# Four planes in place of interleaved residues: output layout, send granularity, early statistics and the side of the bias

## The chip, the cores and the metric

The kernel runs on one core of a Trainium2 chip. A core has a matrix engine (PE, with its weight loads listed as PEld), three elementwise engines (DVE, ACT and POOL) and a sync engine (SP) which in this kernel issues nearly all transfers between the on-chip memory and the device memory. The metric is device time in microseconds. "Span" is the time from the first to the last instruction in one profiled execution.

## The reference

The input `x` has four images of 128 channels and 96 x 96 pixels, in float32. The layer is `x + conv(gn(x))`, where `gn` is a group norm over 32 groups. `conv` reads each image as four sequences of 9216 pixels (rows forward and backward, columns forward and backward), runs the same small network over each, and merges the four results with a 1x1 product:

```
seq_h = flat
seq_v = flat[:, :, order_v]
seq_all = concatenate([seq_h, seq_h[:, :, ::-1], seq_v, seq_v[:, :, ::-1]], axis=0)
...
t = _grouped1x1(x, in_proj_w, in_proj_b, G);  u, gate = t[:, :HID], t[:, HID:]
u = depthwise_conv5(silu(u))
s = _conv1x1(u, ssm_in_w);  a = DMIN + (DMAX - DMIN) * sigmoid(...)
bb = tanh(...);  cc = tanh(...)
hst = exp(prefix) * cumsum(bb * s * exp(-prefix));   prefix = cumsum(log(a))
u = u + _conv1x1(cc * hst + ssm_d * s, ssm_out_w)
u = _grouped1x1(u * sigmoid(gate), mix_w, mix_b, G)
y = _conv1x1(u, out_proj_w, out_proj_b)
...
out = x + einsum('oc,bchw->bohw', fuse_w, concat(h_fwd, h_rev, v_fwd, v_rev)) + fuse_b
```

So every output pixel is the input pixel plus four contributions, one a direction, plus one constant a channel.

## The kernel before, in words

**Phases, steps, pairs.** For each image `b` there are two phases: `V`, which takes the two column sequences, and `H`, which takes the two row sequences. The forward sequence is side `s = 0`, the backward one `s = 1`. A phase has six steps of 16 lines (`NS = 6`, `LN = 16`), and a step has four pairs, one for each residue of the position modulo four, in the order `TURN = (1, 2, 3, 0)`. A pair is the work of both sides for one residue of one step, 384 elements a channel (`N = 384`). There are 192 pairs, numbered `t`; the first six run in `pair(t)`, the others in `pair_on(t)`, and `tail()` ends the kernel. The order of all instructions on each engine is the order in which the program is written (a manual schedule); nothing is moved by a planner. Semaphores for data dependences are put in by the framework.

**What a pair does.** PE runs the input projection of a pair four ahead (`front`, lines 499 to 530), the depthwise convolution of half of the channels as products with banded matrices (`conv`, `conv_less`, line 130), the four small projections (`proj`, line 130), the gates (line 536), the output of the scan (line 556) and the merged output product (`accumulate`, line 130). DVE runs the convolution taps of the other half of the channels (`taps`, line 725), copies of `u` in the first six pairs (line 891), the edge term (line 672), the scan (line 800) and the gating (line 619). ACT runs the nonlinear functions and copies out of PSUM. POOL runs the small products around the scan (lines 773, 774, 806, 807, 809) and the addition into the accumulator (line 852).

**The accumulator.** `acc` holds one whole image on chip, `x` at first, and the four directions are added into it. It is laid out as lines, then residues of the column, then columns: `[P, HH, R, M]`, with `M = 24`. The host brings `x` into the same layout and turns the output back. Each unit's product goes from PSUM through ACT into a buffer `ys` (lines 833 and 835) and is added into `acc` by POOL seven pairs after the unit's own pair. In an H phase one unit's addition covers 16 lines of one residue, runs of 24 elements that lie 96 apart. In a V phase it covers all lines of one residue and four columns of each residue: 24 x 4 runs of four elements. In the H phase ACT also adds the constant of the output (`b_fin`) on side `s = 0`, in the same instruction that copies (line 833); side 1 is a plain copy (line 835). In the last pairs DVE adds straight from PSUM (lines 850, 852, 1135, 1137).

**Sends and reloads.** A block of 16 lines is finished when the second half of an H phase has added its fourth residue (`k == 3`). Then four transfers of 384 KB (two halves of each side's block, 3072 contiguous bytes a partition) go to `done`; `send()` issues them at the start of the next pair (line 815), or at the end of the pair for the last block of an image, and two pairs later (`k == 1`, or `late`, the pair in which the next image's first products are made) the same blocks of the next image's `x` are loaded (line 947). A V addition of the next image touches all lines, so it needs all of these loads. In the last step of the program the transfers are issued at the end (line 1140).

**Statistics of the next image.** The group norm of image `b + 1` is gathered during the V phase of image `b`, from chunks of 384 elements a channel which are loaded on the side into three buffers (`load_chunks`, line 424) and read by DVE (`stats_chunks`, line 430). `chunks_of(t)` says which chunks belong to pair `t`: two in each third and fourth pair of a step. The loads are issued up to two pairs ahead, as soon as a buffer is free. In `pair(t)` DVE's order is: taps of `t`, copies of `u` of `t` (line 891), scan, chunk statistics of `t`; then the taps of `t + 1`.

**The start.** The first image is loaded in chunks and its statistics are taken at once; then `keep_silu` (line 486) sends four 770 KB blocks to device memory at about the time pair 0 begins. All transfers of SP go through one queue in program order: `x_in` loads (lines 297 and 315), `edge` stores (line 657), chunks, gates.

The lines of the core of the addition:

```
        if bu["order"] == "V":
            part = acc.rearrange("p (m q) r c -> p m q r c", q=R)[
                :, :, p, :, bass.ds(st * LN // R, LN // R)
            ]
            y = y.rearrange("p (c r m) -> p m r c", r=R, m=M)
        else:
            part = acc[:, bass.ts(st, LN), p, :]
```

Of the kernel before, what the change touches and what calls it, by code (L numbers as in the profile page):

```python
# [42 lines left out]
F32 = mybir.dt.float32  # L43
# [4 lines left out]
P = 128  # L48
B, DIM, HH, WW = 4, 128, 96, 96
L = HH * WW  # L50
# [6 lines left out]
R = 4  # L57
LN = 16
NS = HH // LN
N = LN * WW // R  # L60
M = WW // R
LAG = 6
UB = 8
NP = NS * R
TURN = (1, 2, 3, 0)
# [3 lines left out]
def conv_preact_kernel(  # L69
# [14 lines left out]
    ps = ctx.enter_context(tc.tile_pool(name="psum", bufs=1, space=bass.MemoryType.PSUM))  # L84
    dp = ctx.enter_context(tc.tile_pool(name="kept", bufs=1, space=bass.MemoryType.DRAM))

    acc = big.tile([P, HH, R, M], F32, name="acc")
    accf = acc.rearrange("p h r m -> p (h r m)")
    x_in = [big.tile([P, R, N + 1], F32, name=f"x_in{s}") for s in range(2)]


# [319 lines left out]
    def chunks_of(t):  # L411

        un = units[min(2 * t, NU - 2)]
        st, k = divmod(t % NP, R)
        if un["order"] == "V" and un["b"] + 1 < B and k > 1:
            return [(un["b"] + 1, 4 * st + 2 * (k - 2) + e) for e in range(2)]
        return []

    def load_chunks(t):
        for b, c in chunks_of(t - 1) + chunks_of(t) + chunks_of(t + 1):  # L420
            if (b, c) not in loaded and len(chunks) < 3:
                loaded.add((b, c))
                chunks[b, c] = wk.tile([P, SC], F32, tag="xs", bufs=3, name=f"xs_{b}_{c}")
                nc.sync.dma_start(chunks[b, c], xr[b, :, bass.ts(c, SC)])
# [140 lines left out]
    def under(bi, s):  # L565

        if bi + s == 0:
            return
        seeded.add((bi, s))
        nc.scalar.copy(psum[:, ssm(bi, s) : ssm(bi, s) + 2, :N], us[bi][:, s])  # L570
# [239 lines left out]

    done, reload = [], []

    def send():
        for b, r in done:
            nc.sync.dma_start(out[b, :, r], accf[:, r])
            if b + 1 < B:
                reload.append((b + 1, r))
        done.clear()

    def accumulate(bu, bk, adder=nc.gpsimd, last=False):  # L820

        b, s, p, st = bu["b"], bu["s"], bu["p"], bu["st"]
        py = bank(bk)
        direct = last and (s == 1 or bu["order"] == "H")
        for j in range(2):
            for c in range(4):
                mm(py, c, w_fin[:, bu["dir"], j, 32 * c : 32 * c + 32], bu["v"][:, j, :],
                   j == 0, j == 1)
        y = py[:, :N]
        if not direct:  # L830
            ys = wk.tile([P, N], F32, tag="ys", bufs=4, name=f"ys_{bu['id']}")
            if s == 0 and bu["order"] == "H":
                nc.scalar.activation(ys, y, AF.Identity, bias=b_fin)  # L833
            else:
                nc.scalar.copy(ys, y)  # L835
            y = ys
        if s == 1:
            y, p, st = y[:, ::-1], R - 1 - p, NS - 1 - st
        if bu["order"] == "V":
            part = acc.rearrange("p (m q) r c -> p m q r c", q=R)[  # L840
                :, :, p, :, bass.ds(st * LN // R, LN // R)
            ]
            y = y.rearrange("p (c r m) -> p m r c", r=R, m=M)
        else:
            part = acc[:, bass.ts(st, LN), p, :]
            y = y.rearrange("p (h m) -> p h m", m=M)

        def add():
            if direct and s == 0:
                adder.scalar_tensor_tensor(part, y, b_fin, part, ALU.add, ALU.add)  # L850
            else:
                adder.tensor_add(part, y, part)  # L852
            if bu["order"] == "H" and bu["st"] >= NS // 2 and bu["end"]:

                done.extend((b, bass.ts(2 * st + e, LN * WW // 2)) for e in range(2))

        return add

# [57 lines left out]
    def pair_on(t):  # L916
# [23 lines left out]
            load_lone(un["step"])  # L940
        if not fronted:
            under(bi, 1)
        if t < end - 2:
            send()
        if len(reload) == 4 and (k == 1 or late):
            for b, r in reload:
                nc.sync.dma_start(accf[:, r], xr[b, :, r])
            reload.clear()
        new_u(i)
        taps(i, range(1, K))  # L950
        conv(i, banks, single)
# [99 lines left out]
    def tail():  # L1051
# [4 lines left out]
        def ssm_out(n):  # L1056
            for s in range(2):
                for j in range(2):
                    out_of(2 * n, s, j)
# [40 lines left out]
        for n in range(first + 2, end - 1):  # L1100
            gate_units(n)
            z_copy(n + 1)
            product(n - 1, 1, 5)
            add()
            product(n, 0, 4)
            ssm_out(n + 1)
        last = 2 * (end - 1)
        half = N // 2
        for s in range(2):
# [8 lines left out]
        for i, s, e in ((-2, 1, 0), (-1, 0, 0), (-1, 0, 1), (-2, 1, 1), (-1, 1, 0), (-1, 1, 1)):  # L1118
# [10 lines left out]
            if s:  # L1129
                lines = HH - lines - LN // 2  # L1130
                y = y[:, ::-1]
            part = acc[:, bass.ds(lines, LN // 2), R - 1 - bu["p"] if s else bu["p"], :]
            y = y.rearrange("p (h m) -> p h m", m=M)
            if s:
                nc.vector.tensor_add(part, y, part)
            else:
                nc.vector.scalar_tensor_tensor(part, y, b_fin, part, ALU.add, ALU.add)
            if bu["end"]:
                region = bass.ds(lines * WW, LN // 2 * WW)
                nc.sync.dma_start(out[bu["b"], :, region], accf[:, region])  # L1140

    def start():
        def filler(n):
# [185 lines left out]
```

## Time and profile before

| | us |
|---|---|
| median of three runs | 1750.28 (1747.95 to 1751.83) |
| the profiled execution's own time | 1753.03 |
| its span | 1750.9 |
| PE busy | 1724.7 |
| DVE, ACT, POOL busy | 1505.8, 1496.0, 1454.4 |

The profile page lists busy time by engine, the span in 40 slices, the transfer queues, the chain of work that ended last, and the costliest groups of instructions. Beside it stand answers of the trace: the windows view gives the busy time of every engine, the granted clock of PE and the share of the transfer engines in a stretch; the timeline lists instructions merged by line (start, time, engine, line, operation, names, count, and in brackets how long the engine had been idle and what it waited for); the view of one tile or line gives the shortest, median and longest duration, what its engine waited for, and for transfers the time from issue to landing. "L852" is line 852 of the kernel before. An engine's idle time between two instructions of 0.02 to 0.1 us is its own issue time.

### The profile page before, as it was taken

The page shows a single profiled execution, that of the slowest core. Times are in us where ns is not written, and L with a number is a line of the kernel's source. Part 1 is how long each engine was busy: PE and PEld are TensorE (multiplying, and loading weights), DVE is VectorE, ACT ScalarE, POOL GpSimd, SP SyncE. Part 2 cuts the span into 40 slices and gives each one's busy share as a digit, 9 for nine tenths or more (in the row PEclk, how much of TensorE's full clock was granted, in tenths as well). Part 3 has the DMA queues.
Part 4 walks back from the last instruction along what each step waited for, and adds up shares of the span by engine and source line. Part 5 has one row for each costly group of instructions (what it writes and reads, how often), then busy time and mean ns, then how long its engine had stood idle before and what let it go on. Part 6 is the DMA issues. An engine that isn't in the chain of part 4 may idle for free.

```text
span 1750.9 us, 54410 instructions
## 1 busy us (share of the span) xinstructions
PE 1724.7 (99%) x22662; PEld 645.5 (37%) x22662; DVE 1505.8 (86%) x1508; ACT 1496.0 (85%) x2543; POOL 1454.4 (83%) x1496
## 2 busy tenths in 40 slices
PE   7999999999999999999999999999999999999998
PEld 3233333433333333334333343334333333333333
DVE  6799988888889998888889999888888888888897
ACT  4688988889888888888888888888888888888875
POOL 3488889888879988978787998898788899887886
PEclk9999999999999999999999999999999999999999
DMA  7645965358885696337897489533897549743454
GB/s 236 198 151 186 309 197 155 116 194 262 279 270 196 230 273 191 124 117 240 256 298 260 147 290 257 159 119 132 273 279 250 196 136 294 213 139 132 147 203 181
DMA packets 164980, 362.68 MB, mean 207 GB/s; under 512 B 16640, under 2 KB 128640, under 8 KB 164736
## 3 DMA queue, kind: packets, MB, share of 16 engines
q1 hardware_dynamic: 164592, 359.17, 63.6%
q8 instruction: 179, 2.93, 0.7%
q14 instruction: 65, 0.53, 0.1%
q10 hardware_dynamic: 144, 0.04, 0.0%
HBM read 220.62 MB, written 138.53 MB: 205 GB/s over the span
## 4 chain that ended last, share of the span: by engine, by line
PE 92%; DVE 2%; POOL 2%; DMA 1%; ACT 1%; issue 1%; SPq 0%; POOLq 0%; DVEq 0%; ACTq 0%
PE psum L130 78%; PE psum L556 8%; PE psum L536 5%; DMA xs<-in_xr 1%; DVE psum L725 1%; PE psum L1144 1%; DMA acc<-in_xr 0%; POOL t L806 0%; POOL t L807 0%; DVE u L619 0%; POOL acc L852 0%; POOL t L774 0%; POOL t L773 0%; SPq L486 0%; ACT psum L570 0%
## 5 line engine op out<-in xcount | busy, mean ns | idle before, releaser
L725 DVE SCALAR_TENSOR_TENSOR psum<-sil,small,psum 128x768 f32<-128x768 f32 x576 | 589.1, 1023 | 41.4 <-ACT psum L723 16.7
L130 PE MATMUL psum<-u,w_fin 128*32 128x384 f32 (+1 forms) x6192 | 541.6, 484 | 1.0 <-ACT ys L833 0.5
L130 PE MATMUL psum<-u,main 128*32 128x384 f32 x6144 | 536.8, 490 | 2.3 <-DVE u L891 2.3
L619 DVE SCALAR_TENSOR_TENSOR u<-gate,psum 128x768 f32<-128x768 f32 x376 | 341.9, 951 | 158.2 <-ACT ys L835 59.8
L852 POOL TENSOR_TENSOR acc<-ys,acc 128x384 f32<-128x384 f32 x375 | 427.3, 1161 | 18.6 <-DMA acc<-in_xr 4.9
L806 POOL TENSOR_TENSOR t<-t,t 64x384 f32<-64x384 f32 (+1 forms) x192 | 275.6, 1435 | 70.7 <-DVE t L800 53.5
L130 PEld LDWEIGHTS psum<-u,w_fin 128*32 128x32 f32 x6192 | 195.7, 110 | 308.9 <-issue 237.9
L570 ACT COPY psum<-u 128x768 f32<-128x768 f32 x383 | 300.3, 799 | 10.4 <-DVE u L619 4.4
L130 PEld LDWEIGHTS psum<-u,main 128*32 128x32 f32 x6144 | 180.4, 110 | 327.3 <-issue 217.2
L130 PE MATMUL psum<-sil,band 128*32 128x384 f32 x3072 | 286.5, 490 | 1.1 <-ACT gate L580 1.1
L773 POOL TENSOR_SCALAR t<-tm 64x384 f32<-64x384 f32 x184 | 173.6, 943 | 117.4 <-ACT tm L762 105.4
L807 POOL TENSOR_TENSOR t<-t,t 64x384 f32<-64x384 f32 (+1 forms) x192 | 234.0, 1219 | 15.1
L723 ACT ACTIVATE psum<-sil,small 128x768 f32<-128x768 f32 x191 | 172.5, 903 | 73.4 <-DVE u L619 64.8
L774 POOL TENSOR_TENSOR t<-t,tm 64x384 f32<-64x384 f32 x192 | 210.5, 1096 | 28.6 <-ACT t L765 13.9
L556 PE MATMUL psum<-t,main 32*128 32x384 f32 x1536 | 226.9, 526 | 3.2 <-ACT psum L570 2.6
L725 DVE SCALAR_TENSOR_TENSOR u<-sil,small,psum 128x768 f32<-128x768 f32 x192 | 194.9, 1015 | 6.8
L506 ACT ACTIVATE sil<-psum,bnorm 128x385 f32<-128x385 f32 x384 | 192.0, 585 | 5.0 <-PE psum L130 2.9
L536 PE MATMUL psum<-x_in,wn 32*128 32x384 f32 x768 | 162.1, 498 | 0.0
L130 PEld LDWEIGHTS psum<-sil,band 128*32 128x32 f32 x3072 | 88.7, 108 | 173.5 <-issue 63.1
L835 ACT COPY ys<-psum 128x384 f32<-128x384 f32 x281 | 129.3, 477 | 21.7 <-PE psum L130 19.0
L762 ACT ACTIVATE tm<-psum,small 128x384 f32<-128x384 f32 x192 | 111.1, 579 | 15.7 <-PE psum L130 6.5
L574 ACT ACTIVATE gate<-psum,bnorm 128x384 f32<-128x384 f32 x152 | 88.0, 581 | 39.8 <-PE psum L536 23.4
(109 smaller groups left out, 1529.6 us busy)
## 6 DMA issues: line engine op xcount, KB each, us to landing
gate<-kept SPq DMA_DIRECT2D x114, 768.0 KB, 5.9
kept<-gate SPq DMA_DIRECT2D x74, 768.0 KB, 3.7
sil<-sil SPq DMA_DIRECT2D x64, 770.0 KB, 7.5
lone<-edge SPq DMA_DIRECT2D x39, 770.0 KB, 7.7
x_in<-in_xs SPq DMA_DIRECT2D x250, 96.2 KB, 3.4
edge<-sil SPq DMA_DIRECT2D x96, 192.5 KB, 4.3
out<-acc SPq DMA_DIRECT2D x48, 384.0 KB, 6.1
acc<-in_xr SPq DMA_DIRECT2D x39, 384.0 KB, 6.8
```

The source lines that it names most:

```text
L130: nc.tensor.matmul(o[r, : rhs.shape[-1]], lhsT, rhs, start=start, stop=stop, skip_group_check=True)
L506: nc.scalar.activation(sils[step][:, s, j, g, :], bank(bk)[:, : N + 1], AF.Silu, bias=bn[:, 1:2] if j else bn[:, 4 + g : 5 + g],)
L536: nc.tensor.matmul(bank(to)[:, :N], stats[un["b"]][0][r, s, :], x_in[s][r, q, off : off + N], start=True, stop=True)
L556: nc.tensor.matmul(bank(ssm(bi, s) + j)[:, :N], w_so[r, bass.ts(j, P)], z[r, :], start=(bi, s) not in seeded, stop=True, skip_group_check= ...
L570: nc.scalar.copy(psum[:, ssm(bi, s) : ssm(bi, s) + 2, :N], us[bi][:, s])
L619: nc.vector.scalar_tensor_tensor(v, g, 1.0, pz, ALU.add, ALU.mult)
L725: nc.vector.scalar_tensor_tensor(us[i][:, :, 1, :] if k == K - 1 else part, src, w_tap[:, k : k + 1], part, ALU.mult, ALU.add,)
L773: nc.gpsimd.tensor_scalar(*decay(i))
L774: nc.gpsimd.tensor_mul(ta[0:64, p, :], tb[0:64, :], tm[0:64, :])
L806: engine.tensor_mul(ta[0:64, p, r], tb[64:P, r], ta[64:P, p, r])
L807: engine.tensor_add(tb[0:64, r], ta[0:64, p, r], tb[0:64, r])
L852: adder.tensor_add(part, y, part)
```

## The change

The change has four parts.

1. **Layout.** `acc`, `x` and the output become four planes, one a residue of the column: `[P, R, HH, M]`. An H addition then covers 384 contiguous elements; a V addition still covers 24 x 4 runs of four elements, with the runs of one residue 96 elements apart and the residues 2304 apart (before: 384 and 24). The host's two transpositions follow.
2. **Sends and reloads.** A block is sent two planes at a time: planes 1 and 2 when `k == 1` is added, planes 0 and 3 when `k == 3` is added. Each transfer is again 384 KB, now two runs of 1536 bytes a partition. Reloads are issued at `k` of 1 or 3 and stand ahead of `send()` in a pair. In the last step of the last image single planes are sent, and in the closing block of `tail()` one plane (or half of one) each.
3. **First statistics.** In the first six pairs one chunk a pair is taken (pairs 2, 3, 4 and 5) where before two were taken in pairs 2 and 3, and only the chunk of that pair is loaded, two pairs ahead.
4. **Output's bias.** `b_fin` is added on side 1 instead of side 0, in ACT's copy and in DVE's direct additions.

```
-    acc = big.tile([P, HH, R, M], F32, name="acc")
-    accf = acc.rearrange("p h r m -> p (h r m)")
+    acc = big.tile([P, R, HH, M], F32, name="acc")
+    accf = acc.rearrange("p r h m -> p (r h m)")
...
         st, k = divmod(t % NP, R)
+        if t < LAG:
+            return [(b0 + 1, t - 2)] if t > 1 else []
...
-        for b, c in chunks_of(t - 1) + chunks_of(t) + chunks_of(t + 1):
+        ahead = chunks_of(t - 1) + chunks_of(t) + chunks_of(t + 1)
+        for b, c in ahead if t > LAG + 1 else chunks_of(t):
...
+    def planes(t, at):
+        r, lines = at
+        return t.rearrange("p (r h m) -> p r h m", r=R, m=M)[:, r, lines, :]
+
     def send():
-        for b, r in done:
-            nc.sync.dma_start(out[b, :, r], accf[:, r])
+        for b, at in done:
+            nc.sync.dma_start(planes(out[b], at), planes(accf, at))
             if b + 1 < B:
-                reload.append((b + 1, r))
+                reload.append((b + 1, at))
...
-            if s == 0 and bu["order"] == "H":
+            if s == 1 and bu["order"] == "H":
                 nc.scalar.activation(ys, y, AF.Identity, bias=b_fin)
...
-            part = acc.rearrange("p (m q) r c -> p m q r c", q=R)[
+            part = acc.rearrange("p r (m q) c -> p m q r c", q=R)[
...
-            part = acc[:, bass.ts(st, LN), p, :]
+            part = acc[:, p, bass.ts(st, LN), :]
...
-            if direct and s == 0:
+            if direct and s == 1 and bu["order"] == "H":
                 adder.scalar_tensor_tensor(part, y, b_fin, part, ALU.add, ALU.add)
...
-            if bu["order"] == "H" and bu["st"] >= NS // 2 and bu["end"]:
-
-                done.extend((b, bass.ts(2 * st + e, LN * WW // 2)) for e in range(2))
+            k = TURN.index(bu["p"])
+            if bu["order"] == "H" and bu["st"] >= NS // 2:
+                lines = bass.ts(st, LN)
+                if b + 1 == B and bu["st"] == NS - 1 and k > 1:
+                    done.append((b, (slice(p, p + 1), lines)))
+                elif k == 1:
+                    done.append((b, (slice(1, 3), lines)))
+                elif k == 3:
+                    done.append((b, (slice(0, R, 3), lines)))
...
+        if k in (1, 3) or late:
+            for b, at in reload:
+                nc.sync.dma_start(planes(accf, at), planes(xr[b], at))
+            reload.clear()
         if t < end - 2:
             send()
-        if len(reload) == 4 and (k == 1 or late):
-            for b, r in reload:
-                nc.sync.dma_start(accf[:, r], xr[b, :, r])
-            reload.clear()
...
             ssm_out(n + 1)
+        send()
...
-            if s:
+            if s == 0:
                 nc.vector.tensor_add(part, y, part)
             else:
                 nc.vector.scalar_tensor_tensor(part, y, b_fin, part, ALU.add, ALU.add)
-            if bu["end"]:
-                region = bass.ds(lines * WW, LN // 2 * WW)
-                nc.sync.dma_start(out[bu["b"], :, region], accf[:, region])
+            if s and bu["end"]:
+                at = slice(r, r + 1), bass.ds(lines, LN // 2)
+            elif e:
+                at = slice(r, r + 1), bass.ts(NS - 1 - bu["st"] if s else bu["st"], LN)
+            else:
+                continue
+            nc.sync.dma_start(planes(out[bu["b"]], at), planes(accf, at))
...
-        "xr": x.reshape(B, DIM, HH, M, R).transpose(0, 1, 2, 4, 3).reshape(B, DIM, L),
+        "xr": x.reshape(B, DIM, HH, M, R).transpose(0, 1, 4, 2, 3).reshape(B, DIM, L),
```

More of the change, by code (lines that the diff above doesn't have):

```diff
@@ L1131, in tail @@
                 y = y[:, ::-1]
-            part = acc[:, bass.ds(lines, LN // 2), R - 1 - bu["p"] if s else bu["p"], :]
+            r = R - 1 - bu["p"] if s else bu["p"]
+            part = acc[:, r, bass.ds(lines, LN // 2), :]
             y = y.rearrange("p (h m) -> p h m", m=M)
-            if s:
+            if s == 0:
                 nc.vector.tensor_add(part, y, part)
@@ L1326 @@
     r = run_bass_kernel_spmd(nc, [arrays], core_ids=[0])
-    y = r.results[0]["out_0"].reshape(B, DIM, HH, R, M)
-    return np.ascontiguousarray(y.transpose(0, 1, 2, 4, 3)).reshape(B, DIM, HH, WW)
+    y = r.results[0]["out_0"].reshape(B, DIM, R, HH, M)
+    return np.ascontiguousarray(y.transpose(0, 1, 3, 4, 2)).reshape(B, DIM, HH, WW)
```

## The prediction

> **What bounds the kernel now.** I read the page's busy times first, then the windows view by stage. The columns of the windows view are the stretch, its length, the busy time of PE, PEld, DVE, ACT and POOL, PE's granted clock, and the share and rate of the transfer engines.
>
> ```profile
> PE 1724.7 (99%) x22662; PEld 645.5 (37%) x22662; DVE 1505.8 (86%) x1508; ACT 1496.0 (85%) x2543; POOL 1454.4 (83%) x1496
> ...
> 0.00:100.00 100.00, 83.95 (x1086) 32.12 (x1086) 71.75 (x111) 59.38 (x110) 43.74 (x73) 0.97 0.74 214
> 100.00:300.00 200.00, 199.99 (x2660) 74.81 (x2656) 180.91 (x180) 175.81 (x301) 180.60 (x184) 1.00 0.62 199
> 900.00:1170.00 270.00, 268.90 (x3644) 99.52 (x3640) 243.48 (x243) 237.31 (x407) 236.76 (x240) 1.00 0.67 214
> 1700.00:1751.00 51.00, 43.16 (x528) 17.18 (x520) 37.99 (x46) 29.19 (x46) 36.58 (x35) 1.00 0.50 181
> ```
>
> PE is the bound: from 100 to 300 us it is never idle. It has 16 us of idle time in the first 100 us, 1.1 us in the stretch 900 to 1170, and 7.8 us in the last 51. The change takes nothing from PE, so it can gain only at these places, and it can lose wherever it makes another engine or a transfer slower than PE. I therefore price four places: the start, the additions on POOL, the change of image, the end. The sums are made against the profiled execution, 1753.03 us (2.1 outside its span of 1750.9); that is 2.75 above the median 1750.28, and I carry the difference over unchanged.
>
> **The start: chunks of the next image's statistics.** This is the timeline of SP, DVE and PE from 34 to 89 us, and the clock in two windows.
>
> ```profile
> 34.48 4.14 SPq L486 DMA_DIRECT2D sil<-sil  x4
> 38.66 4.31 SPq L424 DMA_DIRECT2D xs<-in_xr  x3
> 58.71 0.38 SPq L424 DMA_DIRECT2D xs<-in_xr  x1
> 59.79 2.90 SPq L297 DMA_DIRECT2D x_in<-in_xs  x4
> ...
> 52.16 1.03 DVE L430 BATCH_NORM_STATS2 bn<-xs 128x6 f32<-128x384 f32 x2 [2.54 <-DMA xs<-in_xr]
> 62.11 0.56 DVE L430 BATCH_NORM_STATS2 bn<-xs 128x6 f32<-128x384 f32 x1 [3.43 <-DMA xs<-in_xr]
> 75.03 1.02 DVE L891 COPY u<-psum 128x384 f32<-128x384 f32 x2 [1.27 <-PE psum L130]
> 84.19 1.01 DVE L672 SCALAR_TENSOR_TENSOR u<-lone,small,psum 128x768 f32<-128x768 f32 x1 [2.07 <-PE psum L130]
> ...
> 57.80 2.79 PE L130 MATMUL psum<-u,main 128*32 128x384 f32 x32 [1.62 <-DVE u L891]
> 65.69 0.99 PE L130 MATMUL psum<-x_in,wn 32*32 32x385 f32 x16 [0.82 <-DMA x_in<-in_xs]
> 67.34 4.45 PE L130 MATMUL psum<-u,main 128*32 128x384 f32 x32 [0.66 <-DVE u L891]
> ...
> 64.90:68.30 3.40, 1.95 (x28) 0.73 (x32) 3.33 (x5) 1.45 (x3) 0.00 (x0) 1.00 0.91 242
> 68.30:71.80 3.50, 3.50 (x26) 0.95 (x18) 3.40 (x4) 1.96 (x4) 0.53 (x1) 0.51 0.98 343
> 82.00:85.40 3.40, 3.40 (x24) 0.87 (x16) 1.33 (x3) 2.01 (x4) 3.25 (x4) 0.50 0.44 175
> ```
>
> In pair 2, DVE waits 2.54 us for chunks that were issued right behind 3 MB of stores (line 486), and reads two of them; in pair 3 it waits 3.43 us for a chunk that could be issued only once a buffer was free. The taps of pairs 3 and 4 stand behind these waits, `u` is late, and PE idles 1.62 and 0.66 us; between these it waits 0.82 us for `x_in`.
>
> After the change pair 2 still needs chunk 0, which stands at the same place in the queue, so the 2.54 us stay; only the second read goes (1.03 / 2 = 0.5 us, all of it on the path to PE's 57.80). Pair 3 needs chunk 1, now issued two pairs ahead of its use into a buffer that is free: the 3.43 us go. What is late next in pair 4 is the `x_in` load behind PE's 65.69. Ahead of the loads at 59.79 stood four chunk issues, now three, so they go out earlier by one issue: between 0.38 (the issue at 58.71) and 1.4 us (4.31 / 3). I take 1.2, nearer to the upper end because two of the three issues at 38.66 go, the slow ones, and 384 KB fewer stand ahead in the transfer queue. PE's pair 4 product then starts at about 65.69 + 0.99 - 1.2 = 65.5 instead of 67.34: **1.85 us** (0.38 gives 1.05; 1.4 gives 2.05). DVE gets one more read (0.55 us) in each of pairs 4 and 5; it is hidden in DVE's idle 1.27 and 2.07 us there, and would cost 1.1 us without that cover.
>
> Then the clock. In 64.9 to 68.3 PE was busy 1.95 of 3.4 us, and in the next window it was granted 0.51: the same product took 4.45 instead of 2.79 us. A second such window follows at 82.0. With the waits shorter the first may go, which gives 0 to 1.66 us; I take half, **0.8**, and leave the second as it is, for no wait of this change stands ahead of it. [...] Sum of the start: 2.65 us, from 1.05 to 3.7.
>
> **The additions on POOL.** The rows are POOL in one V step of four pairs (windows view), POOL's pause between two of its instructions in the chain of waits, then durations (shortest/median/longest in ns) of line 852 in V and in H, and of two other POOL operations.
>
> ```profile
> 134.50:169.30 34.80, 34.80 (x424) 13.87 (x416) 32.29 (x33) 30.67 (x51) 31.79 (x29) 1.00 0.48 154
> ...
> 1715.73 0.07 issue
> ...
> L852 POOL TENSOR_TENSOR acc<-ys,acc x14: 1215/1224/1249, 106.9 to 159.7; 128x384 f32<-128x384 f32 x14
> L852 POOL TENSOR_TENSOR acc<-ys,acc x23: 998/1010/2525, 319.1 to 417.7; 128x384 f32<-128x384 f32 x23
> L806 POOL TENSOR_TENSOR t<-t,t x7: 1204/1219/2565, 112.8 to 163.1; 64x384 f32<-64x384 f32 x7
> L774 POOL TENSOR_TENSOR t<-t,tm x12: 1012/1018/1038, 321.2 to 415.8; 64x384 f32<-64x384 f32 x12
> ```
>
> In V, POOL is busy 31.79 of 34.80 us, and about 0.07 us an instruction (29 of them, 2.0 us) is issue time, so about 1.0 us a step is free. A V addition takes 1.22 us, an H one 1.01. Line 774 reads contiguous rows: 1.02. Line 806 reads with a step of four elements, the V addition reads `ys` with a step of 96: both 1.22. So the price is 0.2 for a strided read, and the distance does not show in it. The planes alter only distances in V (innermost run and counts stay), so I take 0 for V; the bounds are -0.2 (as if contiguous, which gains nothing because PE is the bound) and +0.2 (the same price once more). H becomes fully contiguous, as line 774: 0, and POOL has room there. [...]
>
> **The change of image.** The rows are SP at the first change, what POOL waited for at the second, and PE's wait there.
>
> ```profile
> 512.58 2.49 SPq L815 DMA_DIRECT2D out<-acc  x4
> 515.17 4.16 SPq L657 DMA_DIRECT2D edge<-sil  x4
> 519.37 4.26 SPq L947 DMA_DIRECT2D acc<-in_xr  x4
> ...
> POOL acc L852 <- DMA acc<-in_xr: 3.0, 1, 3.0
> PE psum L130 <- ACT gate L580: 1.1, 1, 1.1
> ```
>
> The last reload makes POOL wait 3.0 us, and PE loses 1.1 soon after. After the change four reloads still go out together at `late` (planes 1 and 2 of the last block wait for it too), but only two sends stand ahead of them instead of four: 2.49 / 2 = 1.2 us of issue, so POOL's wait shrinks by about that. I take **0.7** of PE's 1.1 us (0 to 1.1). Elsewhere the new sends and reloads at other pairs put as many transfers on SP, two at a time. A send waits for POOL's additions of the pair before; what is queued behind it is the gate load that DVE needs two pairs later, hidden as today; if POOL were late, that load would be too, and I count it in the second rival below. Runs of 1536 bytes are priced there as well.
>
> **The end.**
>
> ```profile
> L1140 SPq DMA_DIRECT2D out<-acc x4: 332/332/377, 1744.3 to 1746.3; - x4
> DMA to landing us min/median/max: 2.3/2.9/3.3
> L1135 DVE TENSOR_TENSOR acc<-psum,acc x4: 351/358/359, 1743.6 to 1746.0; 128x192 f32<-128x192 f32 x4
> L1137 DVE SCALAR_TENSOR_TENSOR acc<-psum,b_fin,acc x2: 408/408/408, 1743.9 to 1744.2; 128x192 f32<-128x192 f32 x2
> ...
> L815 SPq DMA_DIRECT2D out<-acc x4: 332/424/946, 1737.9 to 1739.2; - x4
> DMA to landing us min/median/max: 2.3/3.2/4.0
> ...
> L833 ACT ACTIVATE ys<-psum,b_fin 128x384 f32<-128x384 f32 x7 | 4.1, 581 | 2.9 <-PE psum L130 2.9
> L835 ACT COPY ys<-psum 128x384 f32<-128x384 f32 x2 | 0.9, 472 | 0.0
> ```
>
> The last of four 384 KB transfers lands 3.3 us after its issue at 1746.3; one with nothing ahead takes 2.3. Four in a row land at 1737.9 + 2.3 = 1740.2 to 1739.2 + 4.0 = 1743.2, so each moves in 1.0 us. The last transfer becomes 96 KB, a quarter: 2.3 - 0.75 = 1.55 if the queue is empty, 2.3 if its predecessors (192, 192, 96 KB) still move. I take 2.0, a gain of 1.3 (1.0 to 1.75). DVE's last addition gets the bias, 0.41 for 0.36 us. In the tail side 0's copies become plain, 0.58 to 0.47, where PE waits for one, and side 1's direct ones a little longer: zero together. The end: **1.3**. In the H phases the bias only changes sides: as many copies of each price, nothing.
>
> **Sum.** 2.65 + 0 + 0.7 + 1.3 = 4.65 us: 1753.03 - 4.65 = 1748.4 in the profile's terms, 1750.28 - 4.65 = **1745.6** as the median. The bounds give 2.05 to 6.55, that is 1743.7 to 1748.2.
>
> **The rivals.** What can be told from no change is 0.2%, 3.5 us.
> 1. Slower: V additions become the bound. POOL has 1.0 us free for eight additions, so it decides from 0.125 us an addition. At the upper bound 0.2 a step grows by 0.6 us, 24 V steps by 14: 1745.6 + 14 = 1760. Against it speaks that 4 and 96 elements cost the same; for it, that no row has a step of 2304 elements. [...]
> 2. Slower: runs of 1536 bytes move badly, and the four reloads and two sends at each change of image take 1 us longer each: 6 - 1.2 = 4.8 us more waiting on POOL, which passes on nearly all beyond about 2 us, three times: 12 to 14 us, 1758. Against: in the start's three chunks, runs of 1536 bytes, the last lands 0.9 us after the first, 0.45 for 192 KB, the speed of the 3072-byte runs.
>
> ```profile
> L424 SPq DMA_DIRECT2D xs<-in_xr x3: 1185/1256/1782, 38.7 to 41.8; - x3
> DMA to landing us min/median/max: 11.3/12.1/13.5
> ```
>
> 3. The start doesn't do what it says: chunk 0's wait stays and `x_in` is as late as before, which leaves 0.5 there: 0.5 + 0.35 + 1.3, about 2.2 us, 1748.1, no change that can be told.
> 4. Both half-clock windows go (1.66 each) and the rest at its good end: 2.05 + 3.3 + 1.1 + 1.75 = 8.2 us, 1742.1.
>
> **How the numbers follow.** The forecast has 0.60 (0.48 of it faster by over 3.5 us, 0.12 within), rival 4 has 0.13, rival 3 has 0.13, rival 1 has 0.08, rival 2 has 0.06. Faster: 0.48 + 0.13 = 0.61; same: 0.12 + 0.13 = 0.25; slower: 0.14. The range runs from just under rival 4 to 2.3 us above rival 3, for the runs shown spread by 3.9 us: 1741.5 to 1750.5; it leaves out rivals 1 and 2 and some of rival 4.
>
> **What would show it.** In the changed profile: no wait of line 430 for `xs` over 1 us after 53 us, PE's pair 4 product near 65.5 us; V additions at 1.22 us; POOL's waits for `acc` loads below 2 us; the last transfer landing about 2 us after its issue. The prediction is wrong if the V additions exceed 1.35 us, if PE shows idle time between 100 and 1650 us that wasn't there, or if the time at which pair 6 starts isn't at least 2 us earlier.

## The result, and the profile after

| | before | after |
|---|---|---|
| median, us | 1750.09 (1747.95 to 1751.83, 5 runs) | 1743.25 (1742.22 to 1744.57, 5 runs) |
| ratio | | 0.9961, 95% interval 0.995 to 0.9973 |
| profiled execution, us | 1753.03 (span 1750.9) | 1742.22 (span 1740.4) |

The change is faster by 6.8 us (4.7 to 8.8 by the interval). A second set of runs of the same kernel, told of below, gives 5.8 us. The forecast was a gain of 4.65 us, to 1745.6. The measured 1743.25 lies in its range of 1741.5 to 1750.5, but the gain of 6.8 is more than the 6.55 us that the bounds of its sum allowed.

The page of the kernel after opens with the busy times, and the windows view holds the stretches that were shown of before (same columns).

```profile
PE 1719.8 (99%) x22662; PEld 648.0 (37%) x22662; DVE 1509.2 (87%) x1508; ACT 1494.9 (86%) x2543; POOL 1449.3 (83%) x1496
...
100.00:300.00 200.00, 200.00 (x2676) 74.89 (x2668) 181.18 (x180) 176.72 (x305) 180.29 (x188) 1.00 0.65 203
900.00:1170.00 270.00, 269.99 (x3640) 100.51 (x3640) 243.23 (x241) 237.58 (x407) 236.52 (x240) 1.00 0.65 209
...
64.90:68.30 3.40, 3.40 (x40) 1.23 (x36) 3.33 (x4) 2.23 (x5) 1.38 (x2) 1.00 0.97 328
68.30:71.80 3.50, 3.50 (x76) 1.06 (x68) 2.96 (x5) 2.70 (x6) 1.77 (x2) 1.00 0.98 326
82.00:85.40 3.40, 3.40 (x56) 0.87 (x56) 3.16 (x4) 3.32 (x7) 2.22 (x3) 1.00 0.40 108
```

PE is still the bound. The 1.1 us that it was idle between 900 and 1170 are gone. At the start both stretches that had run at half clock now have 1.00.

The start in the timeline of SP, DVE and PE:

```profile
37.91 1.78 SPq L427 DMA_DIRECT2D xs<-in_xr  x1
57.44 2.55 SPq L297 DMA_DIRECT2D x_in<-in_xs  x4
...
50.86 0.56 DVE L433 BATCH_NORM_STATS2 bn<-xs 128x6 f32<-128x384 f32 x1 [2.00 <-DMA xs<-in_xr]
56.36 0.55 DVE L433 BATCH_NORM_STATS2 bn<-xs 128x6 f32<-128x384 f32 x1
...
56.03 2.79 PE L130 MATMUL psum<-u,main 128*32 128x384 f32 x32 [0.63 <-DVE u L904]
63.11 0.88 PE L130 MATMUL psum<-x_in,wn 32*32 32x385 f32 x16 [0.41 <-DMA x_in<-in_xs]
63.92 2.79 PE L130 MATMUL psum<-u,main 128*32 128x384 f32 x32
```

One chunk is issued where three were, and one read of DVE waits (2.00 us, pair 2). The read of pair 3 waits for nothing. The four `x_in` loads go out at 57.44 instead of 59.79, and PE's pair 4 product starts at 63.92 instead of 67.34. Of these 3.42 us, 0.8 are an earlier beginning of pair 0 (37.6 instead of 38.4 us).

The additions on POOL (line 859, first in V, then in H: shortest/median/longest in ns), what POOL waited for in the whole run (total, times, longest in us), and the last transfers:

```profile
L859 POOL TENSOR_TENSOR acc<-ys,acc x14: 1215/1221/1237, 100.8 to 153.6; 128x384 f32<-128x384 f32 x14
L859 POOL TENSOR_TENSOR acc<-ys,acc x23: 990/1004/2520, 312.8 to 411.3; 128x384 f32<-128x384 f32 x23
...
POOL acc L859 <- DMA acc<-in_xr: 1.9, 1, 1.9
POOL acc L859 <- DMA lone<-edge: 0.7, 1, 0.7
...
L1159 SPq DMA_DIRECT2D out<-acc x4: 332/336/345, 1735.7 to 1737.5; - x4
L822 SPq DMA_DIRECT2D out<-acc x3: 345/372/372, 1730.8 to 1733.7; - x3
DMA to landing us min/median/max: 1.6/2.4/3.9
```

The V additions cost what they cost before. POOL's longest wait for a reload went from 3.0 to 1.9 us. The last row covers all seven transfers of the two rows above it: the last one lands 1.6 us after its issue (before: 3.3), the 3.9 belongs to the one issued at 1733.7.

### The profile page after: what moved, and what is told of

Its sections match the earlier page's. It is cut to its first block, busy times and chain, and to the rows that moved or that the text cites. A ratio compares the mean times of both kernels' runs of the same rounds, so it can differ in the third digit from the quotient of the medians.

```text
span 1740.4 us, 54418 instructions
## 1 busy us (share of the span) xinstructions
PE 1719.8 (99%) x22662; PEld 648.0 (37%) x22662; DVE 1509.2 (87%) x1508; ACT 1494.9 (86%) x2543; POOL 1449.3 (83%) x1496
## 4 chain that ended last, share of the span: by engine, by line
PE 93%; DVE 2%; POOL 2%; ACT 1%; DMA 1%; issue 1%; SPq 0%; POOLq 0%; DVEq 0%; ACTq 0%
PE psum L130 79%; PE psum L559 8%; PE psum L539 6%; DVE psum L728 1%; PE psum L1163 1%; POOL acc L859 1%; DMA acc<-in_xr 0%; DVE u L622 0%; POOL t L809 0%; ACT psum L573 0%; ACT psum L726 0%; DVE u L728 0%; ACT sil L509 0%; DMA edge<-sil 0%; POOL t L810 0%
## 5 line engine op out<-in xcount | busy, mean ns | idle before, releaser
L859 POOL TENSOR_TENSOR acc<-ys,acc 128x384 f32<-128x384 f32 x375 | 416.5, 1132 | 14.7 <-DMA acc<-in_xr 1.9
L809 POOL TENSOR_TENSOR t<-t,t 64x384 f32<-64x384 f32 (+1 forms) x192 | 282.2, 1470 | 72.3 <-DVE t L803 50.1
L810 POOL TENSOR_TENSOR t<-t,t 64x384 f32<-64x384 f32 (+1 forms) x192 | 233.9, 1218 | 15.1
L559 PEld LDWEIGHTS psum<-t,main 32*128 32x128 f32 x1536 | 94.6, 183 | 75.8 <-issue 41.2
```

Of the source, the lines that this page charges most:

```text
L559: nc.tensor.matmul(bank(ssm(bi, s) + j)[:, :N], w_so[r, bass.ts(j, P)], z[r, :], start=(bi, s) not in seeded, stop=True, skip_group_check= ...
L809: engine.tensor_mul(ta[0:64, p, r], tb[64:P, r], ta[64:P, p, r])
L810: engine.tensor_add(tb[0:64, r], ta[0:64, p, r], tb[0:64, r])
```

## The experiments

What each profile shows, in us, with the pairs taken from the starts of ACT's `tm` (one a pair, line 762 or 765). "Half clock" names where the windows view shows a granted clock of 0.5 between pair 0 and pair 6 or just ahead of it.

| kernel | pairs 2 to 6 | half clock | pairs 32 to 44 (in H) | pair 107 (second change of image) | last product to end |
|---|---|---|---|---|---|
| before | 37.0 | 68.3 and 82.0 | 104.99 | 10.6 | 5.0 |
| statistics alone | 32.5 | 76.8 | 104.99 | 9.7 | 5.0 |
| bias alone | 33.7 | none | 104.72 | 9.7 | 5.0 |
| planes alone | 35.4 | 66.3 | 104.99 | 9.3 | 3.4 |
| after | 31.7 | none | 104.72 | 9.4 | 3.4 |
| after, again | 32.6 | 26.7 to 33.5 and 81.3 | 104.72 | 9.3 | 3.5 |
| sent at once | 32.0 | none | 104.72 | 10.2 | 3.7 |
| whole blocks at the end | 31.8 | none | 104.72 | 9.3 | 6.2 |

**The parts alone.** Each is the kernel before with one part of the change. Here and below the lines of the code that matter are shown.

Statistics alone:

```diff
+        if t < LAG:
+            return [(b0 + 1, t - 2)] if t > 1 else []
...
+        ahead = chunks_of(t - 1) + chunks_of(t) + chunks_of(t + 1)
+        for b, c in ahead if t > LAG + 1 else chunks_of(t):
```

> The kernel before with the early chunks of statistics alone. By the theory of the prediction (three separate places: start, change of image, end) this holds the start's share: pair 6 begins 2.65 us earlier if one window of half clock stays, about 5 us earlier if both go, and nothing changes at the end; so 2.7 to 5 us faster than before. A rival theory says that the half clock at 68 and 82 us has nothing to do with the waits in pairs 2 and 3 and comes and goes from run to run: then the windows are as likely here as before, and the gain is about 1.9 us.

Measured: 1746.44 us against 1750.24, ratio 0.9973 (0.9963 to 0.9983), 3.8 us faster.

Bias alone:

```diff
-            if s == 0 and bu["order"] == "H":
+            if s == 1 and bu["order"] == "H":
                 nc.scalar.activation(ys, y, AF.Identity, bias=b_fin)
...
-            if direct and s == 0:
+            if direct and s == 1 and bu["order"] == "H":
...
-            if s:
+            if s == 0:
                 nc.vector.tensor_add(part, y, part)
```

> The kernel before with the output's bias on the other side alone. The prediction has zero here: at the end 0.1 us saved where PE waits for a copy of side 0, 0.06 us lost where it waits for a direct addition, in the H phases nothing. Expected within 0.5 us of before. A rival says that the longer copy on side 1 holds up the bank that the next projection needs: in every H pair up to 0.1 us, 90 pairs, 9 us slower.

Measured: 1749.0 us, ratio 0.9991 (0.9983 to 1.0), 1.2 us faster, hardly told from nothing by the times. The trace tells it: the windows view with bounds set at the `tm` of pairs 32 and 44, of before and of this kernel.

```profile
318.34:423.33 104.99, 104.98 (x1276) 41.52 (x1272) 88.99 (x85) 93.56 (x154) 86.09 (x88) 1.00 0.59 197
...
315.36:420.09 104.73, 104.73 (x1276) 41.93 (x1272) 88.81 (x85) 93.54 (x155) 85.91 (x88) 1.00 0.59 197
```

The same 1276 products fill 104.98 us in the one and 104.73 in the other, with PE recorded as busy throughout. The difference is the same in the H phases of the first three images and for every kernel of the table; in the fourth it is 0.07 us over the whole phase. So the bias is worth about 3 x 0.27 = 0.8 us.

Planes alone (layout, sends, reloads and tail of the change; statistics and bias as before). The lines are its edit against the changed kernel:

```diff
-        if t < LAG:
-            return [(b0 + 1, t - 2)] if t > 1 else []
...
-            if s == 1 and bu["order"] == "H":
+            if s == 0 and bu["order"] == "H":
```

> The kernel before with the planes and their transfers alone (no early statistics, bias on side 0). By the theory: 0.7 us at the changes of image and 1.3 us at the end, so 2.0 us faster than before, with the waits of pairs 2 and 3 and the half clock as before. A rival says that the planes carry most of the change (shorter bursts on the transfer queue everywhere, 0.8 us at 661 and 1.3 us at 990 us in the trace of before): 3 to 4 us.

Measured: 1747.03 us, ratio 0.9982 (0.9971 to 0.9993), 3.2 us faster. The V additions are unchanged here too, for PE loses nothing in the V steps (busy 199.93 of the 200 us from 100 to 300); the gain is at the second change of image (pair 107) and at the end. The profile of before also has a pair 71 of 10.1 us, at 661 us; every other profile of the table has 9.3 there, those without the planes too, so that is not theirs.

The three parts add up to 3.8 + 1.2 + 3.2 = 8.2 us, more than the 5.8 to 6.8 of the whole, but within what their intervals allow.

**The change once more**, for its second profile:

> The changed kernel once more, on the chip of the next two, as their point of comparison: 0.996 of before.

Measured: 1744.25 us against 1750.05, ratio 0.9964 (0.995 to 0.9979). The profiled execution was 1748.23 us, and the windows view shows why it is late: the columns are as above.

```profile
26.70:30.10 3.40, 3.40 (x56) 1.60 (x40) 0.29 (x5) 3.28 (x8) 0.00 (x0) 0.50 0.19 50
30.10:33.50 3.40, 3.40 (x17) 2.97 (x15) 0.69 (x1) 1.50 (x4) 0.76 (x1) 0.50 0.40 109
...
81.30:84.70 3.40, 3.40 (x24) 0.95 (x16) 1.72 (x3) 2.11 (x4) 3.26 (x4) 0.50 0.50 201
```

The half clock that the first profile of the change was free of is there in the second, at 26.7, which no part of the change touches, and at 81.3. The kernel with the bias alone, whose start is that of before, had none. So the half-clock windows differ from execution to execution of what is the same start.

The mean granted clock of nearly every execution is on record. It is 1.000, which leaves no room for a window of 3.4 us (half of it is 0.001 of 1740 us), in 10 of 12 executions of the change, in 14 of 52 of before (its two later sets) and in 8 of 12 of the planes alone, which have before's start. (A mean below 1.000 does not tell where the half clock was: the profile of the kernel with whole blocks at the end has 0.999 and none between pair 0 and pair 6.) So it is not shown that the change makes half clock rarer. Nor is its gain made by it: the executions at 1.000 alone have medians of 1750.0 before and 1743.0 after, 7.0 us apart.

**The start: chunk 0's wait.** The remaining 2.00 us wait stands behind the 3 MB of stores. Here, in the changed kernel, chunk 0 is issued ahead of them.

```diff
+        load_chunks(2)
         for g in range(R):
             keep_silu(0, g)
```

> The changed kernel with the load of chunk 0 ahead of the four 770 KB stores at the start. By the theory the 2.0 us that DVE still waits in pair 2 go, and with them PE's 0.63 us in pair 3: 0.6 us faster than the changed kernel. A rival says that the load of x_in (PE waits 0.41 us for it in pair 4) is next and no earlier, since SP issues as much ahead of it: then pair 3 gains 0.6 and pair 4 gives it back, no change.

Measured: 1743.5 us, ratio 0.9966 (0.9954 to 0.9979): no gain over the change that can be told. PE had idled only 0.63 and 0.41 us in those pairs of the kernel after, so little was to be had. This kernel's profile says no more, for half clock until 39.6 us began pair 0 seven microseconds late and the transfers were then early in any case. The kernel with the memset below began as late, without chunk 0 ahead of the stores, and both take 30.3 us for pairs 2 to 6.

**The change of image: two planes at a time, or four transfers at once.** The layout stays, but the sends of a block go out together again after `k == 3`.

```diff
-                elif k == 1:
+                elif b + 1 == B:
+                    if k == 1:
+                        done.append((b, (slice(1, 3), lines)))
+                    elif k == 3:
+                        done.append((b, (slice(0, R, 3), lines)))
+                elif k == 3:
                     done.append((b, (slice(1, 3), lines)))
-                elif k == 3:
                     done.append((b, (slice(0, R, 3), lines)))
```

> The changed kernel, but for the first three images all four planes of a block go out together when its fourth residue is added, as before, in four transfers of two runs of 1536 bytes. By the theory POOL's waits for the reloads come back (1.8, 3.0 and 1.9 us before; 0.2, 1.9 and 0.7 in the changed kernel) and PE loses 0.4 to 1.3 us at one change of image: 0.7 us slower than the changed kernel. The second rival of the prediction (short runs move badly) would show here as waits longer than before's, above 4 us. If the layout itself and not the sending carries the gain of the planes, there is no difference.

Measured: 1745.53 us, ratio 0.9973 (0.9957 to 0.9989), 1.3 us above the change's second set, inside the spread of the runs. The waits view of POOL in this kernel:

```profile
POOL acc L859 <- DMA xs<-in_xr: 4.7, 2, 2.6
...
POOL acc L859 <- DMA acc<-in_xr: 1.6, 1, 1.6
```

POOL waits 6.3 us for loads where the change waits 2.8 (1.9, 0.7, and 0.2 not shown), and before 6.7. Pair 107 takes 10.2 us, against 9.3 to 9.4 in the kernels of the table that send two planes at a time. That is the mechanism of the forecast: fewer sends ahead of the reloads, a shorter wait on POOL, and what exceeded about 2 us went on to PE. The profiles line up by POOL's wait at this change of image: pair 107 takes 9.3 us with waits of 0.6 to 0.8, 9.4 with 1.9 (after), 9.7 with 2.3 and 2.4 (bias alone and statistics alone), 10.2 with 2.6 (here) and 10.6 with 3.0 (before).

**The end: all four planes of half a block at once, or single planes.**

```diff
-                if b + 1 == B and bu["st"] == NS - 1 and k > 1:
-                    done.append((b, (slice(p, p + 1), lines)))
+                if b + 1 == B and bu["st"] == NS - 1:
+                    pass
...
-            if s and bu["end"]:
-                at = slice(r, r + 1), bass.ds(lines, LN // 2)
-            elif e:
-                at = slice(r, r + 1), bass.ts(NS - 1 - bu["st"] if s else bu["st"], LN)
-            else:
+            if not bu["end"]:
                 continue
+            at = slice(0, R), bass.ds(lines, LN // 2)
```

> The changed kernel with the last block of the last image sent as before: four transfers of 384 KB (four planes, eight lines) at the very end. By the theory of the prediction the end gives back its 1.3 us (the trace of the changed kernel says 1.7, the last transfer landing 1.6 instead of 3.3 us after its issue): 1.3 to 1.7 us slower than the changed kernel, and all pairs as there. A rival says that the end's gain came from the earlier sends of finished planes, not from the size of the last one; then the last transfers still land one a microsecond, and the time is the same as this theory's; only if neither matters is there no difference.

Measured: 1746.29 us, ratio 0.9979 (0.9969 to 0.9989), 2.0 us above the change's second set. The tile view of `out` at the end of this kernel (issue in ns, then landing):

```profile
L1156 SPq DMA_DIRECT2D out<-acc x4: 597/634/1122, 1735.6 to 1737.7; - x4
DMA to landing us min/median/max: 3.0/3.8/4.5
```

The four closing transfers carry 384 KB again, now as four runs of 768 bytes a partition. Their issue takes 0.63 us instead of 0.33, and they land 1.2 us apart ((1737.7 + 4.5 - 1735.6 - 3.0) / 3) where before it was 1.0. The end takes 6.2 us instead of 3.4, so 2.8 more in the profile where 1.3 to 1.7 were expected, and 1.2 more than before. In planes, then, the sends of the change's last step are not only a gain over before, they are needed. The run holds back the finished planes and enlarges the last transfers at once, so it does not tell which of the two counts, and the rival of its expectation stays untested.

**POOL's free time in a V step.** The prediction's strongest rival on the slow side decides from 0.125 us an addition, 1.0 us in a step of eight. Three kernels put a dose of POOL work ahead of or behind each V addition; nothing that is computed changes.

```diff
                 adder.tensor_add(part, y, part)
+                if bu["order"] == "V":
+                    for _ in range(1):
+                        nc.gpsimd.memset(first_table, 0.0)
```

> The changed kernel with one one-element memset on POOL (0.09 us and 0.07 us of issue, 0.16 together) behind each V addition; its value is used by nothing. The prediction says POOL has 1.0 us free in a V step of eight additions and that 0.125 us an addition decides: 8 x 0.16 = 1.3, so a V step grows from 34.8 to 35.1 us, 24 of them, some 7 us slower. A rival says that POOL's slack in the H phases between takes it up: no pair gets longer.

```diff
+                if bu["order"] == "V":
+                    nc.gpsimd.tensor_copy(ys[:, 0:96], ys[:, 0:96])
                 adder.tensor_add(part, y, part)
```

> The changed kernel with a copy in place of 96 of the 384 columns on POOL ahead of each of the eight additions of a V step; nothing that is computed changes. It asks how much time POOL has left in a V step (four pairs, 34.8 us). The prediction said about 1.0 us, 0.125 us an addition. A copy of 96 columns should cost 0.15 to 0.25 us with what it issues (a quarter of an addition's 1.0 and the issue): eight of them 1.2 to 2.0 us. Prediction's theory: the V step grows by 0.2 to 1.0 us, so 5 to 24 us over 24 steps, and the span is 1746 to 1764 us. Rival: POOL has more time left than the 1.0 us, since an addition that comes late is taken up by the next pair's buffers; then the V step stays at 34.8 us and the span within 2 us of the change's.

The same with `ys[:, 0:384]`:

> The same with a copy of all 384 columns ahead of each V addition, some 0.5 to 0.7 us each with what it issues, 4.0 to 5.6 us a V step. Prediction's theory (1.0 us left): the V step grows by 3.0 to 4.6 us, so 72 to 110 us over 24 steps, and POOL is busy without idle time in the V steps. Rival (far more left, as POOL's additions wait for nobody that PE needs): the V step grows by less than half of that.

Measured: 1748.46 us with the small dose, 1781.81 with 96 columns, 1824.19 with 384, one run each. The memset was worth less than 0.1 us (two additions and their memsets took 2.47 and 2.49 us, two additions of the kernel after 2.40), not the 0.16 that its expectation took, so this dose was too small and the expected 7 us did not come: the V step stayed at 34.8 us. Half clock from 26 to 39.6 us, which began pair 0 seven microseconds late, accounts for most of what its run lost. The tile view of the two copies, and the windows view with bounds at the `tm` of pairs 12 and 16, of after and of the 384-column kernel:

```profile
L860 POOL COPY ys<-ys x13: 254/265/1747, 103.3 to 157.6; 128x96 f32<-128x96 f32 x13
...
L860 POOL COPY ys<-ys x12: 493/505/520, 103.0 to 153.0; 128x384 f32<-128x384 f32 x12
...
135.31:170.07 34.76, 34.76 (x424) 13.90 (x416) 32.24 (x33) 30.62 (x52) 31.73 (x29) 1.00 0.60 201
...
137.74:175.71 37.97, 36.55 (x416) 13.80 (x416) 31.20 (x33) 30.19 (x52) 35.60 (x37) 1.00 0.58 196
```

The copy of 96 columns took 0.27 us, more than the expectation's 0.15 to 0.25 with issue, so its range of 1746 to 1764 us was missed. With the median price the prediction's sum holds: 8 x (0.265 + 0.07) - 1.0 = 1.7 us a V step, 40 us in 24 steps, and the span grew by 39.6 us (1780.0 against 1740.4). For 384 columns: 8 x (0.505 + 0.07) - 1.0 = 3.6, 86 us, and the span grew by 82.1. In the step shown, POOL is full: 35.60 + 37 x 0.07 = 38.2 of 37.97 us, and the step is 3.2 us longer. So about 1.0 to 1.2 us are free by the medians. The means say more: POOL's busy time grew by 66.1 and 112.2 us for 192 copies, 0.34 and 0.58 us each, which by the same sum leaves 1.7 and 1.8 us free. The execution with 384 columns also had a mean granted clock of 0.992, by which an estimated 29 us of it were at half clock (2 x 0.008 x 1822.5), so some of its growth may be the clock's. The growth is not even either: with 96 columns the step shown grew by 1.0 us, and the four pairs from pair 20 and from pair 28 by some 4.5 and 4.3, where PE stops for about 2 us at a time (pair 20 takes 12.1 us, and 9.3 without the copies). The layout cost nothing because its additions kept their 1.22 us; for additions dearer by 0.2 us and more POOL had little room or none.

**Which side's copy PE waits for.** Two kernels add the constant in ACT's copies on both sides of the H phases, or on neither.

```diff
-            if s == 1 and bu["order"] == "H":
+            if bu["order"] == "H":
                 nc.scalar.activation(ys, y, AF.Identity, bias=b_fin)
```

> The changed kernel with the output's constant added in ACT's copies of both sides of the H phases (so it is added twice there; the output is not the reference's). Twelve pairs of an H phase (pairs 32 to 44) took 104.99 us with the longer copy on side 0 and 104.72 with it on side 1. Theory A: PE has to wait for the end of side 0's copies and not for side 1's, so the longer copy (0.58 for 0.48 us) costs 0.27 us per 12 pairs on side 0 and nothing on side 1: here 104.99. Rival B: both sides' copies cost, and what differs is only the order of the two lengths: more than 104.99, about 105.2. Rival C: not the copies but something else that goes with the side: 104.72.

```diff
-            if s == 1 and bu["order"] == "H":
+            if False and bu["order"] == "H":
                 nc.scalar.activation(ys, y, AF.Identity, bias=b_fin)
```

> The changed kernel with plain copies on both sides of the H phases (the output's constant is left out there; the output is not the reference's). Theory A (only side 0's copy lies on PE's path): pairs 32 to 44 take 104.72 us, as with the longer copy on side 1. Rival B (both sides' copies cost): less than 104.72, about 104.45. Rival C (something else that goes with the side): 104.72 here, as in theory A; it is told from A by the run with both.

The windows view with bounds at the `tm` of pairs 32 and 44, first with the constant on both sides, then on neither:

```profile
312.95:418.27 105.32, 105.32 (x1276) 41.89 (x1272) 88.80 (x85) 94.81 (x155) 85.78 (x88) 1.00 0.59 196
...
312.23:416.63 104.40, 104.39 (x1276) 41.68 (x1272) 88.92 (x85) 92.38 (x154) 85.95 (x88) 1.00 0.59 198
```

Neither 104.40, side 1 alone 104.72, side 0 alone 104.99, both 105.32. The costs add: 0.32 us per twelve pairs on side 1 and 0.59 on side 0 (0.32 + 0.59 = 0.91, measured 0.92). Theory A, that only side 0's copy lies on PE's path, falls: the 0.10 us more of a copy that adds the constant (0.58 against 0.48 us) cost PE 0.05 us a pair on side 0 and 0.03 on side 1, on average of these twelve. Over all 24 pairs of the phase the constant on side 1 costs 0.33 us, hardly more than in these twelve, so not every pair pays alike. Which product of PE carries this is not shown; before and after, the waits view lists 3.8 and 3.7 us of the weight load of the gates' product behind these copies, nearly the same for both.

## Why the prediction was right

| step | forecast, us | shown, us | by |
|---|---|---|---|
| start, without the clock | 1.85 | 2.0 | pairs 2 to 6: 33.7 (bias alone, no half clock) to 31.7 (after) |
| start, the clock | 0.8 | not shown | half clock in some profiles of each kind |
| V additions | 0 | 0 | 1.22 us before and after |
| bias in H | 0 | 0.8 | 3 x 0.27 |
| change of image | 0.7 | 0.3 to 1.2 | pair 107, 9.7 to 10.6 against 9.4 |
| end | 1.3 | 1.6 | 5.0 to 3.4 after the last product |
| sum | 4.65 | 4.7 to 5.6 | times: 6.8 and 5.8 |

The sum and the time came out near each other partly by luck. The clock's 0.8 us, which is not shown, stands where the bias's 0.8 us was left out, and the 6.8 us of the first set lie above the sum's own bounds. The spans of the two profiles differ by more, 10.5 us, since before's profiled execution was 2.75 us slower than its median: 6.0 by pair 6, 0.7 at pair 71, 1.2 at pair 107, 0.8 in the H phases, 1.6 at the end and 0.2 elsewhere.

**The start** went by the steps given. The 2.5 us wait for chunk 0 stayed at 2.0, the 3.43 us wait went, and `x_in` was what was late next, by 0.41 us. The loads went out 2.35 us earlier, 1.6 of it net of the earlier beginning, where 1.2 was taken. Net of that beginning PE's pair 4 product is 2.6 us earlier: more than the 1.85, but before's profile had its own waits, and the comparison without half clock gives 2.0. That is one profile of before's start; the six of the early statistics without half clock take 31.3 to 32.5 us for these pairs, so 1.1 to 2.4. The extra reads in pairs 4 and 5 stayed hidden. Pair 6 began 6.0 us earlier, three times the bound named, and half of that was the clock.

**The clock.** The 0.8 us was taken as half of the first window, which the shorter waits might remove, and the second window was said to stay. By their places the profiles fit this. The first window stands behind PE's waits for `u` and `x_in` (68.3 us before, 66.3 with the planes alone): two of the three profiles with before's start have it, and none of the eleven with the early statistics. The second stands 1.2 to 1.7 us behind a wait of PE for ACT's `shared`, 0.15 us long, that all fourteen profiles have. One of the three shows it (82.0 us before), and three of the eleven do. In the profile of the kernel with the statistics alone:

```profile
73.40:76.80 3.40, 3.25 (x44) 0.94 (x44) 3.29 (x5) 3.33 (x8) 3.17 (x4) 0.99 0.46 129
76.80:80.20 3.40, 3.40 (x24) 0.95 (x16) 1.60 (x2) 2.18 (x4) 3.26 (x4) 0.50 0.50 202
```

PE was busy 3.25 of the 3.40 us ahead of that window. In the kernel after, PE is busy 3.25 us in the same stretch too, and the 3.40 us behind it have 1.00, so this idle time alone did not bring the half clock. What the first window was worth is not shown, for 8 of 12 executions of the planes alone had before's waits and no half clock at all. By estimate, from the product of 4.45 us in before's first window against 2.79 at full clock, a window that comes or goes moves an execution by 1.7 us, and the forecast should have carried it as spread instead of as a term.

**The additions on POOL**: right in the price. The runs with the copies put the free time at 1.0 to 1.8 us a step, so the rival's point of decision, 0.125 us an addition, would lie between 0.13 and 0.23. The row stayed at 1.22 us, with its largest step at 2304 elements.

**The bias in H** was the term that was wrong, and the reason given for it the step that failed: "as many copies of each price, nothing" counted the copies and assumed that a copy costs PE the same on either side. On side 0 it costs 0.59 us per twelve pairs, on side 1 0.32.

**The change of image** gained 0.3 to 1.2 us where 0.7 was taken, and only at the second change, where PE had its 1.1 us. **The end** gained 0.3 more than taken, since the last 96 KB landed 1.6 us after their issue, where 2.0 was chosen. That is the 1.55 of the case with an empty queue, though the queue was not empty: the three transfers ahead landed 0.5 to 1.2 us after that issue. So the 2.3 us of the other case did not hold.

**The rivals.** V additions that become the bound did not come, since their price stayed. Short runs did not slow the reloads: POOL's wait went down, from 6.7 to 2.8 us, not up. The start did what it said. The case that both half-clock windows go is what the first profile looks like, but the second profile has one again, so the change does not do it every time. The sum of the shown parts is 0.2 to 2.1 us short of the two measured gains, and 1.4 to 2.3 short of the 7.0 us between the executions at full clock, so half clock does not explain the rest. At full clock the statistics alone (5 executions, median 1746.5) and the planes alone (8, median 1746.8) gain 3.5 and 3.2 us, each more than the profiles show for its places, 2.0 and 1.9 to 2.8. Where the rest comes from stays open.

## What to carry to other kernels

Where PE is full, an instruction of another engine can still cost it a share of its length (here 0.03 to 0.05 us a pair for 0.10 us more of a copy), and which of two like instructions carries the extra work can matter; count what waits behind each, not how many there are. Before a layout changes an engine's accesses, work out how much time per step that engine has left, since here 1 to 2 us in 35 decided between nothing and 40 us. What differs from one profile to the next of the same code, as the granted clock here, belongs in the range and not in the sum.

## What the runs showed of the hardware that was not expected

- Half-clock windows of 3.4 us, or multiples of it, stood at 26, 66, 68, 77, 81 and 82 us in different profiles, one of them behind a stretch in which PE was busy 3.25 of 3.40 us. Those at 77 to 82 stood 1.2 to 1.7 us behind a wait of PE of 0.15 us that ten other profiles have without a window.
- A V addition with planes 2304 elements apart costs 1.22 us, as with 24; strided against contiguous was 1.22 to 1.00.
- Sends of 384 KB land 1.0 us apart with runs of 3072 bytes and 1.2 with runs of 768, and the issue takes 0.33 and 0.63 us.
- A longer copy on ACT (0.58 for 0.48 us) stretched twelve pairs of PE by 0.32 to 0.59 us although PE is recorded as busy without a gap.
